# Layer 3's normalisation in eight VectorE steps, and a newly planned order, in an eight-part decoder kernel

## The chip, the cores and the metric

The kernel runs on one core of a Trainium2 chip. The metric is the time of one execution on the device in microseconds (us), as the median of several runs. Five engines work side by side, each through its own queue in order: TensorE (PE in the profile; PEld are its weight loads), VectorE (DVE), ScalarE (ACT), GpSimd (POOL) and SyncE (SP, which here only issues DMAs). The kernel before takes 1987.3 us (three runs, 1986.98 to 1990.2).

## The reference

x holds 128 batches of 64 tokens of 128 numbers, and a context of the same shape. Four layers follow one another; each adds an attention on the context and then a feed-forward part to x, and both read layer-normalised x:

```
x = x + L0_xattn(norm(x), ctx)   16 heads, softmax
x = x + L0_ffn(norm(x))          8 experts, gated by thresholded softmax
x = x + L1_xattn(ctx, norm(x))   16 heads, relative bias, softmax
x = x + L1_ffn(norm(x))          1 of 2 experts and a shared one, relu
x = x + L2_xattn(norm(x), ctx)   16 heads, masked products without softmax
x = x + L2_ffn(norm(x))          1 of 7 experts and a shared one, swiglu
x = x + L3_xattn(norm(x), ctx)   1 head; its result is normalised, scaled, shifted
x = x + L3_ffn(norm(x))          attention in which 2 of 4 experts give Wq, Wk, Wv
```

The changed code is the end of L3_xattn. With y the attention's result, mu and var its mean and variance over 128 numbers, gamma and beta two rows of weights:

```
x = x + (y - mu) * rsqrt(var + 1e-5) * gamma + beta
```

## The kernel before, in words

**Tiles.** The 8192 tokens are 16 groups of 512. The x of a group stays in SBUF as `xg[g]`, 128 partitions by 4 tiles (t) by 128 numbers. All arithmetic is in float32. The layers' parts are functions that append operations for one group: `attention` (layers 0 to 2), `l0f`, `l1f`, `route`, `shared`, `block`, `gather` (layer 2's feed-forward part, in two halves of 12 and 4 groups, with expert blocks gathered through DRAM), `l3x` (layer 3's attention, one call per group), `mix` and `l3f` (layer 3's feed-forward part, with weights chosen per batch; `load` on L1723 fetches those of a batch by DMA from SP).

**How the order comes about.** `op` appends an operation (a few instructions on one engine) to a `Plan`: the engine, a duration that the author gives in us, what it reads and writes, a priority. `alt` names another engine that may do it. `Plan.order` then works as a list scheduler: for each engine it looks at the ready operations, takes those that could start within `WINDOW` of the earliest, and of them the one of lowest priority; it compares the engines' choices by start (plus `ALT` times the duration where there is an alternative), books the engine and the buffer slot, and goes on. The priority is that of the group and stage plus a number from the table `PRI`, by the operation's name. `spec` gives how many buffers of a kind there are; an operation that needs one waits for a free slot. `port=True` says that a VectorE operation is to be planned only once POOL is free. The durations decide nothing but this order; each engine then runs its queue in it, and semaphores hold an instruction until its inputs are there.

**Around the change.** In `l3x` the values come out of two PSUM banks (`av`, L1538), are scaled into `y` (a buffer of kind "o", L1550), and `stats` (L536, L538) takes mean and variance of y on VectorE. `pow_rs` (L544, L545) makes rs = (var + eps)^-0.5 on POOL. Then, before the change, come: `norm`, four TENSOR_SCALARs on VectorE (L1562), y = (y - mu) * rs, one per tile; a product with gamma over the whole group on POOL (L1570); `add_row` (L610), x + beta, on POOL or VectorE; the sum x + y on POOL (L1574); and `stats` of the new x, for layer 3's feed-forward part. L1464 (in `gather`), L1399 (in `shared`) and L1078 (in `l0f`) are SCALAR_TENSOR_TENSORs on VectorE in the same shape, out = (in0 op scalar) op in1: L1464 takes both tensors from SBUF, L1399 and L1078 one from PSUM, and the four of an L1078 row add into the same tile of x one after another. L779 is the maximum over scores, L794 their subtraction on POOL, L785 the exponential, L809 the transposes of the scores, L821 the product with the values, L755 the scores, L1734 the projections with the chosen weights. L1199 to L1244 are the steps of routing (`r2` to `r5`), L1625 to L1637 the choice of experts in layer 3 (`choose`).

Of the kernel before, what the change touches and what calls it, by code (L numbers as in the profile page):

```python
# [16 lines left out]
ALU = mybir.AluOpType  # L17
# [3 lines left out]
P = 128  # L21
# [44 lines left out]
SKEW, SKEW3, ALT, WINDOW = 15.0, 12.0, 1.160527449, 0.268996472  # L66
# [5 lines left out]
    "block0 block <lambda> 4": -4, "block0 block tr 0": 37, "block0 dma fn 4": 30.5,  # L72
    "block0 swiglu <lambda> 0": 3.5, "block0 swiglu <lambda> 1": 35.5, "block0 swiglu <lambda> 2": -1,
    "block0 swiglu down 0": 20, "block1 block <lambda> 1": 13.5, "block1 block <lambda> 4": -12.5,
    "block1 block tr 0": -22.5, "block1 dma fn 4": 71, "block1 swiglu <lambda> 0": 4,
    "block1 swiglu <lambda> 1": 41, "block1 swiglu <lambda> 2": -32, "block1 swiglu down 0": 1,
    "gather0 gather <lambda> 3": 3.5, "gather0 gather fn 2": 6.5, "gather0 stats fn 2": -0.5,
    "gather1 gather <lambda> 3": 78, "gather1 gather fn 2": 29.5, "gather1 stats fn 2": -3.5,
    "l0f copy_out fn 1": 3, "l0f l0f <lambda> 0": 9, "l0f l0f <lambda> 1": 9.5, "l0f l0f <lambda> 2": -145,
    "l0f l0f acc 2": -123.5, "l0f l0f eb 0": 46.5, "l0f l0f g1 2": 43.5, "l0f l0f g2 2": 41.5,  # L80
    "l0f ln_xn fn 1": 17.5, "l0f logits fn 0": 18.5, "l0f pow_rs fn 3": -4, "l0f stats fn 2": -39,
    "l0f transpose4 fn 0": 59.5, "l1f add_row <lambda> 3": 12.5, "l1f copy_out fn 1": -43.5,
    "l1f l1f <lambda> 0": 196, "l1f l1f <lambda> 2": 55.5, "l1f l1f <lambda> 3": 48, "l1f l1f choose 2": 11.5,
    "l1f l1f down 0": 360, "l1f l1f relu 1": 32, "l1f ln_xn fn 1": -12, "l1f logits fn 0": 5, "l1f pow_rs fn 3": 7,
    "l1f stats fn 2": 0.5, "l1f transpose4 fn 0": 45.5, "l3f0 attend av 0": 41.5, "l3f0 attend tr 0": -4.5,
    "l3f0 copy_out fn 1": -52, "l3f0 dma fn 4": -9.5, "l3f0 exp_ <lambda> 1": 25, "l3f0 fill_kbd fn 4": 56,
    "l3f0 l3f <lambda> 1": 2, "l3f0 l3f <lambda> 2": 17, "l3f0 l3f <lambda> 3": 106, "l3f0 l3f b_v 3": 51.5,
    "l3f0 l3f evac 1": -131, "l3f0 l3f load 4": -2, "l3f0 l3f project 0": -36.5, "l3f0 l3f put 2": -15,
    "l3f0 maximum fn 2": 40, "l3f0 normalise fn 2": 4, "l3f0 out_proj <lambda> 2": 36, "l3f0 out_proj fn 0": 11,
    "l3f0 scores fn 0": -58, "l3f0 shift fn 3": -1, "l3f1 attend av 0": 1, "l3f1 attend tr 0": -22,  # L90
    "l3f1 copy_out fn 1": 8.5, "l3f1 dma fn 4": -3, "l3f1 exp_ <lambda> 1": 14, "l3f1 fill_kbd fn 4": -18,
    "l3f1 l3f <lambda> 1": -2, "l3f1 l3f <lambda> 2": -13.5, "l3f1 l3f <lambda> 3": 4, "l3f1 l3f b_v 3": 9.5,
    "l3f1 l3f evac 1": 12.5, "l3f1 l3f load 4": -13.5, "l3f1 l3f project 0": -58, "l3f1 l3f put 2": -8,
    "l3f1 maximum fn 2": 4, "l3f1 normalise fn 2": -2, "l3f1 out_proj <lambda> 2": 4, "l3f1 out_proj fn 0": -4.5,
    "l3f1 scores fn 0": -26, "l3f1 shift fn 3": -6.5, "l3x0 add_row <lambda> 3": 8, "l3x0 copy_out fn 1": -36,
    "l3x0 dma fn 4": 61.5, "l3x0 l3x <lambda> 1": 166, "l3x0 l3x <lambda> 2": -5.5, "l3x0 l3x <lambda> 3": -10.5,
    "l3x0 l3x av 0": 28.5, "l3x0 l3x norm 2": -21.5, "l3x0 l3x sc 0": 7, "l3x0 l3x sums 2": 33,
    "l3x0 l3x tr 0": -17.5, "l3x0 ln_xn fn 1": 14, "l3x0 pow_rs fn 3": 12, "l3x0 stats fn 2": 9,
    "l3x0 transpose4 fn 0": 15, "l3x1 add_row <lambda> 3": 3.5, "l3x1 copy_out fn 1": -38, "l3x1 dma fn 4": 97,
    "l3x1 l3x <lambda> 1": 36.5, "l3x1 l3x <lambda> 2": 8, "l3x1 l3x <lambda> 3": -2, "l3x1 l3x av 0": 13.5,  # L100
    "l3x1 l3x sc 0": 26, "l3x1 l3x sums 2": -28.5, "l3x1 l3x tr 0": 7.5, "l3x1 ln_xn fn 1": -1,
    "l3x1 pow_rs fn 3": -3, "l3x1 stats fn 2": -1, "l3x1 transpose4 fn 0": -1, "mix0 add_row <lambda> 3": 26.5,
    "mix0 copy_out fn 1": -64, "mix0 ln_xn fn 1": -3.5, "mix0 mix <lambda> 0": 54.5, "mix0 mix <lambda> 1": 18.5,
    "mix0 mix <lambda> 2": -29.5, "mix0 mix b3mm 0": 37.5, "mix0 mix choose 2": 81, "mix0 mix put 2": 27.5,
    "mix0 mix spread_ 0": 101, "mix0 mix weigh 2": -76, "mix0 pow_rs fn 3": -17.5, "mix0 transpose4 fn 0": 38,
    "mix1 add_row <lambda> 3": 42, "mix1 copy_out fn 1": -14.5, "mix1 ln_xn fn 1": 3.5, "mix1 mix <lambda> 0": 16,
    "mix1 mix <lambda> 1": 10.5, "mix1 mix <lambda> 2": -26.5, "mix1 mix b3mm 0": 1.5, "mix1 mix choose 2": 5.5,
    "mix1 mix put 2": 28, "mix1 mix spread_ 0": 15.5, "mix1 mix weigh 2": -25.5, "mix1 pow_rs fn 3": 2.5,
    "mix1 transpose4 fn 0": -0.5, "route copy_out fn 1": -98.5, "route dma fn 4": 0.5, "route ln_xn fn 1": 51.5,
    "route pow_rs fn 3": 13, "route route <lambda> 1": 2, "route route <lambda> 2": -25,  # L110
    "route route <lambda> 3": 48.5, "route route count 0": -3, "route route r2 2": -22, "route route r3 2": 8,
    "route route r4 2": 11.5, "route route r5 2": -1.5, "route route take 2": -4.5, "route stats fn 2": -19.5,
    "route transpose4 fn 0": 7, "shared0 copy_out fn 1": 10.5, "shared0 ln_xn fn 1": 10.5,
    "shared0 shared fn 2": 11.5, "shared0 swiglu <lambda> 0": 11, "shared0 swiglu <lambda> 1": 8.5,
    "shared0 swiglu <lambda> 2": 7, "shared0 swiglu down 0": 20.5, "shared0 transpose4 fn 0": 3.5,
    "shared1 copy_out fn 1": -16, "shared1 ln_xn fn 1": 24, "shared1 shared fn 2": -7,
    "shared1 swiglu <lambda> 0": 11, "shared1 swiglu <lambda> 1": -2.5, "shared1 swiglu <lambda> 2": 1,
    "shared1 swiglu down 0": 6.5, "shared1 transpose4 fn 0": 21.5, "table0 table <lambda> 0": 26,
    "table0 table b1 2": -3.5, "table0 table b2 2": 28, "table1 table <lambda> 0": 16, "table1 table b1 2": 2,
    "table1 table b2 2": 9.5, "x0 add_row <lambda> 3": 27, "x0 attend av 0": -6, "x0 attend tr 0": 9.5,  # L120
    "x0 attention <lambda> 2": -1.5, "x0 attention <lambda> 3": 26, "x0 copy_out fn 1": -102, "x0 dma fn 4": 504.5,
    "x0 exp_ <lambda> 1": -9, "x0 fill_kbd fn 4": -5, "x0 ln_xn fn 1": 19.5, "x0 maximum fn 2": 70,
    "x0 normalise fn 2": -88.5, "x0 out_proj <lambda> 2": -40.5, "x0 out_proj fn 0": -25.5, "x0 pow_rs fn 3": 4,
    "x0 proj <lambda> 0": 32.5, "x0 proj fn 1": -32, "x0 scores fn 0": 12, "x0 shift fn 3": -2,
    "x0 stats fn 2": -30, "x0 transpose4 fn 0": 10, "x0 vproj evac 1": -2, "x0 vproj fn 0": 73,
    "x1 attend av 0": 33, "x1 attend tr 0": 6.5, "x1 attention <lambda> 2": -35, "x1 attention <lambda> 3": 11,
    "x1 copy_out fn 1": -28.5, "x1 dma fn 4": 501.5, "x1 exp_ <lambda> 1": 10, "x1 fill_kbd fn 4": 5,
    "x1 ln_xn fn 1": 95.5, "x1 maximum fn 2": 10.5, "x1 normalise fn 2": -46.5, "x1 out_proj <lambda> 2": -103,
    "x1 out_proj fn 0": -1, "x1 pow_rs fn 3": 2, "x1 proj <lambda> 0": 24, "x1 proj fn 1": -1,
    "x1 scores fn 0": 83.5, "x1 shift fn 3": -14, "x1 stats fn 2": -15.5, "x1 transpose4 fn 0": 8,  # L130
    "x1 vproj evac 1": -1, "x1 vproj fn 0": 9.5, "x2 add_row <lambda> 3": 0.5, "x2 attention <lambda> 2": -46,
    "x2 attention <lambda> 3": 90.5, "x2 copy_out fn 1": -11.5, "x2 dma fn 4": 506, "x2 fill_kbd fn 4": 3.5,
    "x2 ln_xn fn 1": -3, "x2 out_proj <lambda> 2": -34, "x2 out_proj fn 0": -0.5, "x2 pow_rs fn 3": 8,
    "x2 product fn 0": -45, "x2 proj <lambda> 0": -13, "x2 proj fn 1": -9.5, "x2 scores fn 0": -13,
    "x2 stats fn 2": -15.5, "x2 transpose4 fn 0": 29, "x2 vproj_by_batch evac 2": -93.5,
    "x2 vproj_by_batch fn 0": -44, " b2_row b2_row 2": 2.5, " dma fn 4": 497, " lambda <lambda> 0": 32.5,
    " lambda <lambda> 2": -29.5, " lambda <lambda> 3": 14.5, " rel_mm rel_mm 0": -11.5,
# [162 lines left out]
def kernel(ctx: ExitStack, tc: tile.TileContext, a: dict, out: bass.AP):  # L300
# [93 lines left out]
    def g4(ap):  # L394
        return ap.rearrange("p (t d) -> p t d", t=TP)
# [1560 lines left out]
```

## Time and profile before

| what | us |
|---|---|
| median of three runs | 1987.3 |
| the profiled execution's own time | 1991.25 |
| its span, first to last instruction | 1989.5 |
| PE busy | 1811.3 |
| VectorE busy | 1546.2 |
| ScalarE busy | 1084.5 |
| POOL busy | 1022.3 |
| `norm`, L1562, 64 instructions, VectorE | 26.5 |
| product with gamma, L1570, 16 instructions, POOL | 20.5 |
| sum into x, L1574, 16 instructions, POOL | 20.3 |
| all bn_stats of x, L536, 512 instructions, VectorE | 110.5 |

Busy times of different engines overlap; one engine's busy time can't exceed the span. The page's second part gives busy tenths in 40 slices, each some 50 us: layers 0 to 2 fill roughly the first 1200 us, the expert blocks the next 300, layer 3 runs from about 1500 to the end. A row of the timeline names start, length, engine, line, operation, output<-inputs, shapes and how many instructions are merged, and in brackets for how long the engine had been idle and what ended that. Its length runs from the first start to the last end, so four instructions of 343 ns may take 1.13 us together: one starts before the one ahead has fully ended.

### The profile page before, as it was taken

How to read it: one execution, taken by the hardware profiler on the slowest of the kernel's cores; microseconds unless marked ns; L12 is line 12 of the kernel's file. 1: busy time of each engine (PE TensorE's matmuls, PEld its weight loads, DVE VectorE, ACT ScalarE, POOL GpSimd, SP SyncE). 2: the span in 40 equal slices, each digit the busy share in tenths (PEclk: the TensorE clock that was granted, in tenths of full speed). 3: DMA queues.
4: the chain of work that ended last, by engine and by line, in shares of the span. 5: the costliest groups of instructions: out<-in, count | busy, mean ns of one | idle time of the engine just before them, and what ended most of it. 6: DMA issues, size and time to landing. Idle time of an engine off the chain costs nothing.

```text
span 1989.5 us, 66420 instructions
## 1 busy us (share of the span) xinstructions
PE 1811.3 (91%) x27506; PEld 1306.3 (66%) x27506; DVE 1546.2 (78%) x4023; ACT 1084.5 (55%) x2032; POOL 1022.3 (51%) x1331
## 2 busy tenths in 40 slices
PE   6878999999999999999999999999999897888886
PEld 5544756665765666765666677878756676677665
DVE  5989897878798987798887865354577877988776
ACT  2544755555655564556564554344455666765664
POOL 4635745554555664457654471020388767755231
PEclk8989999999999999999999999999999999998898
DMA  6200001011011010001101012444424576545561
GB/s 187 79 13 27 27 26 30 13 30 41 19 34 46 24 35 29 27 26 50 29 25 33 22 37 84 124 136 122 119 74 124 153 237 198 173 148 167 174 196 55
DMA packets 139229, 158.73 MB, mean 80 GB/s; under 512 B 40836, under 2 KB 98096, under 8 KB 138928
## 3 DMA queue, kind: packets, MB, share of 16 engines
q1 hardware_dynamic: 134832, 146.09, 24.2%
q0 software_dynamic: 4096, 8.40, 1.4%
q8 instruction: 216, 3.54, 0.8%
q14 instruction: 85, 0.70, 0.1%
HBM read 121.66 MB, written 15.99 MB: 69 GB/s over the span
## 4 chain that ended last, share of the span: by engine, by line
PE 50%; DVE 25%; POOL 7%; issue 7%; ACT 5%; DMA 4%; SPq 2%; POOLq 0%; DVEq 0%; ACTq 0%
PE b L1353 8%; PE b L1144 6%; PE b L809 5%; DVE x L1078 4%; POOL s L794 4%; DVE mx L779 4%; PE S L755 4%; PE b L1125 4%; PE b L1382 4%; PE b L1068 3%; PE b L638 3%; PE b L1734 3%; PE b L821 2%; PE b L864 2%; DVE s L967 2%
## 5 line engine op out<-in xcount | busy, mean ns | idle before, releaser
L794 POOL TENSOR_TENSOR s<-s,mx 128x512 f32<-128x512 f32 x320 | 324.0, 1047 | 224.1 <-DVE mx L779 190.5
L593 ACT COPY p<-b 128x512 f32<-128x512 f32 x370 | 199.4, 591 | 143.2 <-PE b L809 128.2
L809 PE MATMUL b<-ident,s 128*128 128x128 f32 x1536 | 217.1, 291 | 45.9 <-ACT s L785 33.7
L785 ACT ACTIVATE s<-s 128x2048 f32<-128x2048 f32 x96 | 183.8, 1914 | 114.2 <-POOL s L794 84.2
L809 PEld LDWEIGHTS b<-ident,s 128*128 128x128 f32 x1536 | 180.2, 149 | 91.0 <-ACT s L785 55.2
L563 ACT ACTIVATE xn<-x,nmr,rstd 128x128 f32<-128x128 f32 x472 | 194.4, 487 | 26.8 <-POOL nmr L548 25.2
L1078 DVE SCALAR_TENSOR_TENSOR x<-b,gt,x 128x128 f32<-128x128 f32 x512 | 177.8, 347 | 30.5 <-PE b L1068 14.3
L544 POOL TENSOR_SCALAR ve<-mv 128x4 f32<-128x4 f32 x144 | 34.8, 242 | 319.4 <-DVE mv L538 304.8
L755 PE MATMUL S<-kbd,q 32*64 32x256 f32 x4096 | 152.8, 404 | 42.6 <-DMA kbd<-k 20.4
L1144 PEld LDWEIGHTS b<-fw,hbig 128*128 128x128 f32 x1536 | 180.6, 195 | 10.4 <-issue 9.4
L1144 PE MATMUL b<-fw,hbig 128*128 128x128 f32 x1536 | 186.3, 279 | 0.0
L779 DVE TENSOR_REDUCE mx<-s 128x32 f32<-128x2048 f32 x80 | 181.8, 2274 | 3.6 <-ACT s L1786 2.9
L1370 DVE TENSOR_TENSOR hbig<-fm,b 128x256 f32<-128x256 f32 (+2 forms) x180 | 85.4, 487 | 102.0 <-ACT fm L1365 75.1
L1134 ACT ACTIVATE hbig<-b,cols 128x512 f32<-128x512 f32 x164 | 111.3, 685 | 82.8 <-PE b L1125 81.8
L1068 PE MATMUL b<-mats,fx 128*128 128x512 f32 x256 | 140.5, 632 | 1.9 <-DVE x L1078 1.5
L545 POOL TENSOR_TENSOR rstd<-ve,mhalf 128x4 f32<-128x4 f32 x128 | 133.6, 1044 | 10.6
L755 PEld LDWEIGHTS S<-kbd,q 32*64 32x64 f32 x4096 | 82.1, 137 | 83.2 <-DMA kbd<-k 19.2
L1353 PE MATMUL b<-fx,hbig 128*128 128x256 f32 (+1 forms) x528 | 129.1, 393 | 4.7 <-ACT fx L1441 1.0
L1365 ACT ACTIVATE fm<-b 128x256 f32<-128x256 f32 (+2 forms) x180 | 76.7, 438 | 101.0 <-PE b L1353 91.9
L821 PEld LDWEIGHTS b<-p,vaug 128*32 128x32 f32 x6144 | 97.1, 111 | 50.6 <-issue 23.5
L821 PE MATMUL b<-p,vaug 128*32 128x64 f32 x6144 | 123.3, 225 | 6.5 <-issue 3.6
L1125 PE MATMUL b<-fm,fw 128*128 128x512 f32 x256 | 125.1, 606 | 0.6 <-DVE x L1078 0.3
(292 smaller groups left out, 3870.2 us busy)
## 6 DMA issues: line engine op xcount, KB each, us to landing
fw<-in_l_w SPq DMA_DIRECT2D x64, 384.0 KB
vaug<-in_l_w SPq DMA_DIRECT2D x64, 384.0 KB
hbig<-in_l_w SPq DMA_DIRECT2D x44, 544.0 KB
c<-in_ctxT SPq DMA_DIRECT2D x64, 256.0 KB
kbd<-k SPq DMA_DIRECT2D x256, 64.0 KB
q<-xs_d SPq DMA_DIRECT2D x44, 128.0 KB
ys_d<-o SPq DMA_DIRECT2D x44, 128.0 KB
x<-in_x SPq DMA_DIRECT2D x32, 128.0 KB
```

Of the source, the lines that this page charges most:

```text
L563: A.activation(y[:, t, :], xg[g][:, t, :], AF.Identity, bias=nmr[:, g, n], scale=rstd[:, g, n])
L593: A.copy(tl(dst), tl(b))
L755: T.matmul(ps[64 * i : 64 * i + 64, r, u * 256 : u * 256 + 256], lhsT=qT[row, 64 * b : 64 * b + 64], rhs=kbd[row, :, 64 * b : 64 * b + 64] ...
L779: V.tensor_reduce(tl(mxr), heads(y), AX.X, ALU.max)
L794: G.tensor_tensor(y, y, bc(tl(mxr)[:, h], 2, [P, n, S]), ALU.subtract)
L809: T.transpose(tl(b)[:, r * P : (r + 1) * P], tl(s)[:, c : c + P], ident)
L821: T.matmul(tl(po)[32 * r : 32 * r + 32, c : c + 64], lhsT=vaugs[kv.slot][:, w0 : w0 + 32], rhs=tl(ps[p])[:, r * P + 64 * i : r * P + 64 * ...
L1068: lambda t=t, u=u, pe=pe: T.matmul(tl(pe), lhsT=tl(xnT)[:, t * P : (t + 1) * P], rhs=mats[:, M_E0 + 4 * u : M_E0 + 4 * u + 4, :], start=Tr ...
L1078: V.scalar_tensor_tensor(xg[g][:, t, :], tl(pe)[:, e * D : (e + 1) * D], w[:, t, 4 * u + e : 4 * u + e + 1], xg[g][:, t, :], ALU.mult, ALU ...
L1125: lambda n=n, src=src, ph=ph: T.matmul(tl(ph), lhsT=fw[:, n * P : (n + 1) * P], rhs=tl(src), start=True, stop=True),
L1144: T.matmul(tl(py)[:, t * P : (t + 1) * P], lhsT=tl(hs[n])[:, t * P : (t + 1) * P], rhs=w2f[:, n, :], start=(n == 0), stop=(n == 11),)
L1353: T.matmul(tl(ps)[0:n, at : at + m], lhsT=w()[:, off + c * P : off + c * P + n], rhs=tl(xT)[:, 0:m], start=True, stop=True,)
```

## The change

First, the end of `l3x`. The product with gamma and the sum into x leave POOL. `norm` is now eight SCALAR_TENSOR_TENSORs on VectorE, two per tile: y = (y - mu) * gamma, then x = y * rs + x. The row beta is added to x ahead of it. The norm writes x and y, is planned at 1.75, and no longer waits for POOL in the plan.

```diff
+        add_row(g, R_BETA, pri)
+
         def norm():
             for t in range(TP):
-                V.tensor_scalar(
-                    g4(tl(y))[:, t, :], g4(tl(y))[:, t, :], mv3[:, g, t, 0:1], rs3[:, g, t : t + 1],
-                    ALU.subtract, ALU.mult,
+                y_, x_ = g4(tl(y))[:, t, :], xg[g][:, t, :]
+                V.scalar_tensor_tensor(
+                    y_, y_, mv3[:, g, t, 0:1], rows[:, R_GAMMA : R_GAMMA + D], ALU.subtract, ALU.mult
                 )
-
-        op(DVE, 1.3, norm, r=[R3, M3], w=[y], pri=pri, port=True)
-        op(
-            POOL, 1.27,
-            lambda: G.tensor_tensor(g4(tl(y)), g4(tl(y)), bc(rows[:, R_GAMMA : R_GAMMA + D], 1, [P, TP, D]), ALU.mult),
-            r=[W["rows"]], w=[y], pri=pri,
-        )
-        add_row(g, R_BETA, pri)
-        op(POOL, 1.27, lambda: G.tensor_tensor(xg[g], xg[g], g4(tl(y)), ALU.add), r=[y], w=[X[g]], pri=pri)
+                V.scalar_tensor_tensor(x_, y_, rs3[:, g, t : t + 1], x_, ALU.mult, ALU.add)
+
+        op(DVE, 1.75, norm, r=[R3, M3, W["rows"]], w=[y, X[g]], pri=pri)
         stats(g, pri)
```

Second, the durations that the plan is given (m is 4 for most calls of route):

```diff
-        op(DVE, 1.1 + 0.45 * m, r2, r=[C], w=[rt], pri=pri)
+        op(DVE, 1.1 + 0.65 * m, r2, r=[C], w=[rt], pri=pri)
-        op(DVE, 0.2 + 0.8 * m, r3, w=[rt, RUN[half]], pri=pri - 1)
+        op(DVE, 0.2 + 1.0 * m, r3, w=[rt, RUN[half]], pri=pri - 1)
-        op(DVE, 0.7 + 0.4 * m, r4, r=[rank, W["misc2"]], w=[rt], p=[POS[half]], pri=pri - 1)
+        op(DVE, 0.6 + 0.2 * m, r4, r=[rank, W["misc2"]], w=[rt], p=[POS[half]], pri=pri - 1)
-        op(DVE, 1.4 + 0.2 * m, r5, w=[rt, *WSH[g0 : g0 + m]], pri=pri)
+        op(DVE, 1.1 + 0.1 * m, r5, w=[rt, *WSH[g0 : g0 + m]], pri=pri)
-        op(PE, 1.0, av, r=[pT, cv], w=pos_, hold=[y], pri=pri, mode="v")
+        op(PE, 0.65, av, r=[pT, cv], w=pos_, hold=[y], pri=pri, mode="v")
-        op(DVE, 4.2, choose, r=[W["rows"], C], w=[sel, pg], pri=pri)
+        op(DVE, 2.7, choose, r=[W["rows"], C], w=[sel, pg], pri=pri)
-                op(SP, 0.95, load, r=[TAB3[g // GATE]], w=[wt], pri=pri - 1, lat=3.5, after=[*mark["l1f"], *mark["x2"]])
+                op(SP, 0.95, load, r=[TAB3[g // GATE]], w=[wt], pri=pri - 1, lat=4.3, after=[*mark["l1f"], *mark["x2"]])
-            op(ACT, 0.5, evac, r=[b, *VA], p=[va], hold=[kv], pri=pri, alt=[(DVE, 0.5)])
+            op(ACT, 0.6, evac, r=[b, *VA], p=[va], hold=[kv], pri=pri, alt=[(DVE, 0.5)])
```

Third, the numbers of buffers and of the planner. In `spec`, q goes from 2 to 4, k from 3 to 2, o from 3 to 2, fm from 4 to 3, p from 5 to 4, mb from 3 to 4, mx from 12 to 16, st from 4 to 18. Every entry of `PRI` is new (252 entries before, 244 after); two lines of some 100 show the kind:

```diff
-SKEW, SKEW3, ALT, WINDOW = 15.0, 12.0, 1.160527449, 0.268996472
+SKEW, SKEW3, ALT, WINDOW = 15.0, 12.0, 1.255146523, 0.172540063
...
-    "l3x0 l3x av 0": 28.5, "l3x0 l3x norm 2": -21.5, "l3x0 l3x sc 0": 7, "l3x0 l3x sums 2": 33,
+    "l3x0 l3x av 0": 13.5, "l3x0 l3x norm 2": 8, "l3x0 l3x sc 0": -35, "l3x0 l3x sums 2": 14.5,
```

The priorities of the DMAs of context, masks and x (`x0 dma`, `x1 dma`, `x2 dma` and `dma`) go from about 500 to about 735. With these numbers the order of the instructions on every engine and in every queue is made anew.

## The prediction

> **What bounds the kernel now.** I read the page's busy line and slices first, then busy time by stretches, then what TensorE waits for, and last single rows in order of time.
>
> ```profile
> span 1989.5 us, 66420 instructions
> PE 1811.3 (91%) x27506; PEld 1306.3 (66%) x27506; DVE 1546.2 (78%) x4023; ACT 1084.5 (55%) x2032; POOL 1022.3 (51%) x1331
> ...
> PE   6878999999999999999999999999999897888886
> ```
>
> TensorE (PE) is busy for 91% of the span: a full TensorE with gaps at both ends. As long as its work stays the same, at most 1989.5 - 1811.3 = 178 us can be won. The stretches say where the gaps lie (columns: stretch, length, busy PE, PEld, DVE, ACT, POOL, granted clock, DMA share, GB/s).
>
> ```profile
> 1200.00:1300.00 100.00, 98.83 (x893) 78.66 (x892) 45.98 (x127) 40.10 (x94) 8.60 (x14) 1.00 0.36 107
> ...
> 1500.00:1600.00 100.00, 87.36 (x682) 67.54 (x680) 79.35 (x328) 62.06 (x144) 79.89 (x114) 0.95 0.51 144
> 1600.00:1700.00 100.00, 84.94 (x1713) 69.00 (x1713) 78.41 (x211) 63.29 (x136) 68.41 (x82) 0.95 0.66 211
> 1700.00:1800.00 100.00, 84.25 (x2024) 69.70 (x2025) 91.46 (x242) 68.27 (x137) 66.34 (x84) 0.97 0.55 176
> 1800.00:1900.00 100.00, 82.12 (x1937) 69.18 (x1939) 76.13 (x164) 60.10 (x102) 45.39 (x49) 0.90 0.54 171
> ```
>
> TensorE idles 43.5 us before 200, 40.6 from 200 to 1200, 6.1 from 1200 to 1500, 61.3 from 1500 to 1900 and 27.2 in the last 90: layer 3, where the edited step runs (1498 to 1814), holds a third of all gaps, and the tail a seventh. What ended TensorE's waits from 1500 to 1830, the longest five (columns: waiting tile and line, releaser, total us, times, longest):
>
> ```profile
> PE S L755 <- DMA kbd<-k: 5.4, 3, 3.6
> PE S L755 <- DVE s L1778: 5.0, 5, 1.5
> PE b L1382 <- DVE hbig L1370: 3.1, 3, 2.1
> PE b L809 <- ACT p L593: 3.1, 6, 1.9
> PE b L1734 <- DVE tn L841: 2.4, 1, 2.4
> ```
>
> Over all rows of that answer VectorE (DVE) ends 24.5 of the 48.9 idle us there, half. GpSimd (POOL) ends 0.7. So time taken from POOL buys little directly, and time put on VectorE is paid at some 50%.
>
> **The step itself.** Its three old parts, undisturbed, and the three prices for the new one:
>
> ```profile
> 1552.66 1.11 DVE L1562 TENSOR_SCALAR o<-o,mv,rs 128x128 f32<-128x128 f32 x4
> ...
> 1553.85 1.27 POOL L1570 TENSOR_TENSOR o<-o,rows 128x512 f32<-128x512 f32 x1 [2.89 <-DVE o L1562]
> ...
> 1555.19 1.27 POOL L1574 TENSOR_TENSOR x<-x,o 128x512 f32<-128x512 f32 x1
> ```
>
> ```profile
> 500.63 1.51 DVE L1078 SCALAR_TENSOR_TENSOR x<-b,gt,x 128x128 f32<-128x128 f32 x4
> ...
> 1439.21 1.13 DVE L1464 SCALAR_TENSOR_TENSOR x<-k,tok,x 128x128 f32<-128x128 f32 x4
> ...
> 1690.35 3.94 DVE L1464 SCALAR_TENSOR_TENSOR x<-k,tok,x 128x128 f32<-128x128 f32 x4
> ...
> 1690.92 2.60 POOL L610 TENSOR_TENSOR x<-x,rows 128x512 f32<-128x512 f32 x2
> ```
>
> *Removed.* Per group 1.11 us of VectorE and two POOL products; from the first start (1552.66) to the last end (1556.46) 3.80 us. The 64 TENSOR_SCALARs hold 26.5 us of VectorE in all, 8.7 over 16 x 1.11, since some were stretched. POOL loses 20.5 + 20.3 = 40.8 us, and two hand-overs between engines, for which POOL waited 14.0 us and VectorE 3.3.
>
> *Added.* Eight SCALAR_TENSOR_TENSORs per group. Independent ones (L1464) take 1.13 us for four: pitch (1.13 - 0.343)/3 = 0.262. Where each reads what the one before wrote (L1078), four take 1.51: pitch (1.51 - 0.347)/3 = 0.388. The new loop alternates: the second of a pair reads the y that the first wrote, the next pair is independent. So 4 x 0.388 + 3 x 0.262 + 0.343 = 2.68 us, at least 7 x 0.262 + 0.343 = 2.18 if nothing is held. I take 2.68, since L1078 is the nearest row with such a dependence. VectorE then holds 16 x 2.68 = 42.9 us, 16.4 more than now; with stalls like the present 8.7, 25.1 more. From 1500 to 1830 it would be busy some 293 to 302 us of 330 instead of 276.8.
>
> *On the path.* The chain of work that ended last, cut to 1490 to 1835, holds 7.9 us of L1562 (2.3% of 345) and 5.1 of the two POOL products: 13.0. The new step, on that chain in the same share, holds 7.9 x 42.9/26.5 = 12.8. I cost the fused step at 0: what the two POOL products give back, VectorE takes. Ends: -13 if it leaves the chain, +25 if every added VectorE us shows. The 3.3 us in which stats waited for L1574 go; late next are the stats themselves, in order behind the longer norm on VectorE.
>
> *The wait it adds.* The norm now writes x, so it waits for the beta row (L610, 1.27 us, on POOL for 62 of 80). Behind it on VectorE stand stats, maxima and evacuations. The row needs only the old x and is now ahead of the norm; POOL's power for rs (L545, 1.05 us), which the norm needs in any case, covers most of it. Price 0, or 16 x 1.27 = 20 if beta comes last each time; that lies within the +25.
>
> *The shared port.* The four-instruction row at 1690 took 3.94 us instead of 1.13 while two POOL sums ran; 1.60 and 2.31 stand in two other groups. The L1399 form, whose one tensor is in PSUM, never passed 353 ns. The Trainium skill (SBUF — State Buffer, Who interferes with whom) gives the reason, and it speaks against this edit: a VectorE instruction with two tensors in SBUF contends with a GpSimd instruction that reads SBUF, and the later one stands still till the other is done. By that rule the eight new instructions all are exposed, and one POOL sum met per group would add an estimated 16 x 1.27 = 20 us; by the rows of L1464 (4.5 us of stalls on 18.1 of work) the new step would gather 11, with 40.8 us less of POOL to meet. The sum above uses 8.7, the present step's.
>
> **The new order.** Every instruction after the start may move, on SP's and POOL's queues too; no row prices that, so I bound it. Ends: all gaps after 1500 closed (-88), or layer 3's VectorE-ended waits doubled (+24). For a gain speak the planner's new costs, checked against rows: choose ran from 1582.72 to 1585.29, 2.57 (old cost 4.2, new 2.7); the running sums of routing 596.35 to 600.47, 4.1 (3.4, now 4.2); r4 604.87 to 605.94, 1.1 (2.3, now 1.4); r2 592.65 to 596.4, 3.7 (2.9, now 3.7); sixteen av matmuls 0.60 to 0.84 (1.0, now 0.65); weight loads on the chain 4.7 to 5.7 (3.5, now 4.3). All move toward the trace, and the chain's longest pieces in layer 3 are such loads. Against it stands one: the norm is planned at 1.75 less 0.09 = 1.66, and I expect 2.68. So VectorE runs 1.0 late per group, 16 in all; at 50% this costs 8 us. I take a quarter of the 88.5 idle us after 1500 as regained, 22: between nothing and all, nearer nothing since the old order came of the same planner and waits are many and small (none above passes 5.4 us in sum). The changed buffers (q, mb, mx, st more; k, o, fm, p fewer) I cost at 0: no wait above is for a free buffer by name; each costs at most one such wait (2 us) per group in a stage if the cover goes.
>
> **Sum.** 0 - 22 + 8 = -14 us. The profiled execution took 1991.25 (span 1989.5 and 1.75 around it), so 1977.3; the median of the runs, 1987.3, is 4.0 below that execution, and the same step gives 1973.
>
> **Rivals.** *A, the forecast (0.50):* layer 3's gaps shrink, 1973; its own range 1952 to 1983. *B, the whole order improves (0.08):* a third of the 84 idle us before 1200 goes as well, 1973 - 28 = 1945. For it: SP, priorities and buffers change everywhere; against it, 200 to 1200 is 96% busy. *C, the step doesn't shorten (0.08):* a POOL op met each time makes 2.68 + 1.27 = 3.95 against 3.80, and the order regains only that: 1987. *D, VectorE becomes the bound in layer 3 (0.34):* for it speak 91.46 us of 100 at 1700 to 1800 already, and a norm planned a third too short, so that queues behind it shift. Its price is the whole 25 us on VectorE, less the 3.3 of stats' waits that go, with nothing regained by the order: +22, 2009. It decides where the order regains less than what reaches TensorE of those 25: 12 us at the share of 50%, 25 at full share. Against it: VectorE still idles 28 us of the 330 in the sum above.
>
> **How the numbers follow.** About 0.2% (4 us, 1983.3 to 1991.3) is what a measurement here can tell from no change. Faster by more: A and B, 0.58; within: C, 0.08; slower: D, 0.34. The range 1948 to 2012 takes in A, C and the upper end of +25, and leaves out most of B and the worst of D, in which the order loses as well: some 0.2 together.
>
> **What would show it.** Right: eight instructions of some 2.7 us per norm, POOL near 981 us busy, VectorE near 1563 to 1571, TensorE's idle after 1500 down by 10 to 20 us. Wrong: a norm of 2.2 or of 4 us; VectorE over 95% busy between 1700 and 1800 with TensorE's waits on it grown; gaps that moved to the front. One thing would break the sum altogether: an order that changes the 200 to 1500 stretch by more than its 47 idle us suggest.

## The result and the profile after

The changed kernel takes 2000.9 us (median of seven runs, 1997.1 to 2008.2) where the kernel before takes 1987.3 on the same chip: ratio 1.0070, 95% interval 1.0051 to 1.0090, so 14 us slower where 14 us faster was forecast. The case that came nearest is rival D: VectorE's work in layer 3 is paid for. The profiled execution took 1997.25 us, 6.0 more than the profiled one of before, so the two profiles together show less than half of the 14 us. The page of after, busy times and TensorE's slices:

```profile
span 1995.5 us, 66520 instructions
...
PE 1810.9 (91%) x27506; PEld 1312.2 (66%) x27506; DVE 1582.0 (79%) x4090; ACT 1086.4 (54%) x2062; POOL 975.0 (49%) x1294
...
PE   7778999999999999999999999999988888787786
```

TensorE's work is what it was (1810.9 against 1811.3 us). POOL has lost 47.3 us, and VectorE has gained 35.8. The gaps stand where they stood, at both ends, but those at the back are deeper. The stretches, in the same columns as for the kernel before:

```profile
1400.00:1500.00 100.00, 90.48 (x545) 63.10 (x545) 73.31 (x266) 47.27 (x106) 61.83 (x85) 0.97 0.37 106
1500.00:1600.00 100.00, 82.33 (x799) 62.26 (x797) 87.30 (x332) 49.37 (x118) 64.48 (x100) 0.85 0.49 147
1600.00:1700.00 100.00, 86.57 (x1629) 72.06 (x1629) 82.17 (x204) 66.56 (x132) 36.56 (x46) 0.98 0.55 171
1700.00:1800.00 100.00, 77.08 (x1813) 64.39 (x1811) 90.34 (x221) 64.69 (x131) 60.36 (x76) 0.93 0.60 183
1800.00:1900.00 100.00, 80.12 (x1942) 68.54 (x1939) 88.71 (x206) 62.28 (x134) 45.10 (x56) 0.93 0.54 167
```

Add up TensorE's busy time to see where these 6 us went. At 1400 us the new kernel has done 1326.0 us of it and the old one 1314.6: it is 11.4 us ahead. At 1860 it has done 1708.7 against 1715.3: it is 6.5 behind. So 18 us were lost in these 460, most of them layer 3's, where VectorE was busy 388.0 us instead of 366.6. From 1400 to the end, the waits of TensorE that VectorE ended grew from 34.3 to 56.1 us, those that ScalarE ended from 24.6 to 33.9, and those that DMAs ended shrank from 23.5 to 10.7. The longest five from 1500 to 1830:

```profile
PE S L753 <- DVE s L1772: 6.3, 7, 1.5
PE b L1728 <- DVE x L891: 4.2, 1, 4.2
PE b L1380 <- DVE hbig L1368: 4.1, 2, 3.9
PE S L753 <- DMA kbd<-k: 3.4, 3, 1.4
PE b L819 <- DVE hbig L1368: 3.3, 1, 3.3
```

Four of the five name VectorE now (three did before), and three of these come down to a single wait of 3.3 to 4.2 us each: one operation of VectorE came late, once. The longest single wait in the five shown of before was 3.6, for a DMA. The two lines of the new step (busy us, mean ns of one):

```profile
L1566 DVE SCALAR_TENSOR_TENSOR x<-o,rs,x 128x128 f32<-128x128 f32 x64 | 31.2, 488 | 5.2 <-POOL rs L543 2.2
...
L1563 DVE SCALAR_TENSOR_TENSOR o<-o,mv,rows 128x128 f32<-128x128 f32 x64 | 26.4, 412 | 0.1
```

The rows add up to 57.6 us. Neighbours overlap and are counted twice there, as each starts before the one ahead has ended; with the overlaps counted once the step holds VectorE for some 53.7 us. Forecast were 42.9 bare and 51.6 with stalls. Undisturbed a norm takes 2.75 us from first start to last end (1558.21 to 1560.96), close to the 2.68 worked out. At the median lengths (346 and 352 ns) the two rows would add up to 64 x 0.346 + 64 x 0.352 = 44.7 us, so 12.9 us are stalls. One of the stretched norms, and who waits for it:

```profile
1581.41 1.27 POOL L608 TENSOR_TENSOR x<-x,rows 128x512 f32<-128x512 f32 x1
1581.51 1.32 DVE L1566 SCALAR_TENSOR_TENSOR x<-o,rs,x 128x128 f32<-128x128 f32 x1
...
1582.64 2.13 POOL L1698 TENSOR_TENSOR mats<-hbig,mats 128x512 f32<-128x512 f32 x2
1582.75 1.12 DVE L1563 SCALAR_TENSOR_TENSOR o<-o,mv,rows 128x128 f32<-128x128 f32 x1
...
1583.91 1.01 DVE L1566 SCALAR_TENSOR_TENSOR x<-o,rs,x 128x128 f32<-128x128 f32 x1
...
1585.00 1.31 POOL L608 TENSOR_TENSOR x<-x,rows 128x512 f32<-128x512 f32 x1
1585.22 1.23 DVE L1566 SCALAR_TENSOR_TENSOR x<-o,rs,x 128x128 f32<-128x128 f32 x1
...
1587.14 0.42 DVE L1368 TENSOR_TENSOR hbig<-fm,b 96x256 f32<-96x256 f32 x1
...
1587.61 0.38 PE L1380 MATMUL b<-hbig 128*128 128x128 f32 x1 [3.85 <-DVE hbig L1368]
```

Read it downwards. Each instruction takes 0.35 us alone. Four of the eight take 1.01 to 1.32, and each of them starts some 0.1 to 0.2 us after a POOL operation has begun (L1698's row holds two) and ends some 0.15 us after it: VectorE stands until POOL has done. Over all 64 of each line the longest take 1126 and 1391 ns, while the medians stay at 0.35 us: a minority of the instructions makes the stalls. The norm lasts from 1581.04 to 1587.11, 6.07 us. Directly behind it on VectorE stands L1368, and TensorE's matmul of L1380 waits 3.85 us for that. One stretched norm is a wait on TensorE in the very next operation.

### The profile page after: what moved, and what is told of

It is laid out like the page before. It is cut to its first block, busy times and chain, and to the rows that moved or that the text cites. A ratio compares the mean times of both kernels' runs of the same rounds, so it can differ in the third digit from the quotient of the medians.

```text
span 1995.5 us, 66520 instructions
## 1 busy us (share of the span) xinstructions
PE 1810.9 (91%) x27506; PEld 1312.2 (66%) x27506; DVE 1582.0 (79%) x4090; ACT 1086.4 (54%) x2062; POOL 975.0 (49%) x1294
## 3 DMA queue, kind: packets, MB, share of 16 engines
q1 hardware_dynamic: 134832, 146.09, 24.2%
## 4 chain that ended last, share of the span: by engine, by line
PE 48%; DVE 31%; POOL 6%; issue 6%; ACT 4%; DMA 3%; SPq 1%; POOLq 0%; DVEq 0%; ACTq 0%
PE b L1351 8%; PE b L1142 6%; PE b L807 5%; DVE x L1076 4%; PE b L1123 4%; PE b L1380 4%; DVE mx L777 4%; PE S L753 3%; POOL s L792 3%; DVE s L965 2%; PE b L819 2%; PE b L1066 2%; PE b L1728 2%; PE b L636 2%; PE b L581 2%
## 5 line engine op out<-in xcount | busy, mean ns | idle before, releaser
L783 ACT ACTIVATE s<-s 128x2048 f32<-128x2048 f32 x96 | 183.5, 1912 | 121.9 <-POOL s L792 95.4
L753 PE MATMUL S<-kbd,q 32*64 32x256 f32 x4096 | 147.8, 398 | 31.3 <-DVE s L1772 13.1
L1368 DVE TENSOR_TENSOR hbig<-fm,b 128x256 f32<-128x256 f32 (+2 forms) x180 | 85.8, 488 | 104.3 <-ACT fm L1363 77.1
L543 POOL TENSOR_TENSOR rstd<-ve,mhalf 128x4 f32<-128x4 f32 x128 | 133.5, 1043 | 10.7
L1247 POOL DMA_INDIRECT xs_d<-p,rt x64 | 63.3, 990 | 126.4 <-ACT p L561 102.4
```

What stands on the lines that cost most here:

```text
L753: T.matmul(ps[64 * i : 64 * i + 64, r, u * 256 : u * 256 + 256], lhsT=qT[row, 64 * b : 64 * b + 64], rhs=kbd[row, :, 64 * b : 64 * b + 64] ...
L783: op(ACT, 1.92, lambda: A.activation(tl(s), tl(s), AF.Exp), w=[s], pri=pri, mode="exp")
```

## The experiments

Two theories: **S**, the step costs the time, since VectorE's work in layer 3 grows; **O**, the step is nearly free, and the newly made order is worse on the chip. Ratios are to the kernel before on the same chip, with 95% intervals; busy times are those of one profiled execution each; 1 point, a hundredth of the ratio, is some 20 us.

**e1, the step alone.** Before's order, instruction for instruction; the eight instructions stand where the four stood, and the two POOL products are left out of POOL's queue, their sums being in the eight.

```diff
-                V.tensor_scalar(
-                    g4(tl(y))[:, t, :], g4(tl(y))[:, t, :], mv3[:, g, t, 0:1], rs3[:, g, t : t + 1],
-                    ALU.subtract, ALU.mult,
+                y_, x_ = g4(tl(y))[:, t, :], xg[g][:, t, :]
+                V.scalar_tensor_tensor(
+                    y_, y_, mv3[:, g, t, 0:1], rows[:, R_GAMMA : R_GAMMA + D], ALU.subtract, ALU.mult
+                )
+                V.scalar_tensor_tensor(x_, y_, rs3[:, g, t : t + 1], x_, ALU.mult, ALU.add)
...
+            lambda: None,
```

> The order of before, instruction for instruction, with the eight SCALAR_TENSOR_TENSORs in the place of the four TENSOR_SCALARs and without the two POOL products. Theory S (the step: VectorE pays): 16 norms grow from 1.11 us to 2.75 and more, some 26 us of added VectorE time with stalls, of which most reaches the end: 2003 to 2012. Theory O (the order: the step is free, the new plan is worse on the chip): within 0.3% of before, 1981 to 1993.

Measured: 1.0061 (1.0047 to 1.0075), +12 us, between the ranges of S and O. VectorE went up by 19.2 us to 1565.4, POOL down by 41.1. The step by itself brings nearly the whole loss, without any new order. Its rows:

```profile
L1566 DVE SCALAR_TENSOR_TENSOR x<-o,rs,x 128x128 f32<-128x128 f32 x64 | 26.5, 413 | 4.2 <-POOL rs L545 1.3
L1563 DVE SCALAR_TENSOR_TENSOR o<-o,mv,rows 128x128 f32<-128x128 f32 x64 | 25.3, 395 | 0.0
```

They add up to 51.8 us, 7.1 of them stalls. So in this order both the length of the step and VectorE's total came as forecast (51.6, and 1563 to 1571); what they cost did not.

**e2, half of the step in after's order** (first of the two instructions out).

```diff
-                V.scalar_tensor_tensor(
-                    y_, y_, mv3[:, g, t, 0:1], rows[:, R_GAMMA : R_GAMMA + D], ALU.subtract, ALU.mult
-                )
```

> The order of after, with only the second instruction of each pair: x = y * rs + x. The subtraction of the mean and the product with gamma are left out, so the norm is four instructions, about 1.1 us where the plan has 1.66. Theory S: some 35 us of VectorE time go (57.6 busy to about 22), and 70 to 90% of it shows: 1970 to 1980, below before. Theory O: at most half shows, and the new order stays at or above before: 1986 to 1999.

Measured: 0.9933 (0.9915 to 0.9951). Its norm holds 26.2 us in all, 1.64 a group: about what the order was planned for. VectorE is busy 1557.8 us, 24.2 less than in the changed kernel, and the time is 1.37 points, 27 us, less: theory S's range.

**e3, two loops:** four first steps, then four second ones, so that no instruction reads what the one just ahead of it wrote.

```diff
+            for t in range(TP):
+                y_, x_ = g4(tl(y))[:, t, :], xg[g][:, t, :]
                 V.scalar_tensor_tensor(x_, y_, rs3[:, g, t : t + 1], x_, ALU.mult, ALU.add)
```

> The order of after; the norm does its four first steps and then its four second ones, so that no instruction reads what the one ahead of it wrote: 7 x 0.262 + 0.343 = 2.18 us undisturbed instead of 2.75, 9 us less in all. Theory S: 1992 to 1994. Theory O: 1996 to 2001.

Measured: 1.0036 (1.0018 to 1.0054), between the ranges of S and O. The norm's rows shrink from 57.6 to 48.7 us, but part of that is overlap that is no longer counted twice: VectorE as a whole goes from 1582.0 to 1578.2. A third of a point comes back; still slower than before.

**e4, a third instruction per tile**, whose result nobody reads.

```diff
                 V.scalar_tensor_tensor(x_, y_, rs3[:, g, t : t + 1], x_, ALU.mult, ALU.add)
+                V.scalar_tensor_tensor(
+                    y_, y_, mv3[:, g, t, 0:1], rows[:, R_GAMMA : R_GAMMA + D], ALU.subtract, ALU.mult
+                )
```

> The order of after with a third instruction per tile, which writes the dead y again: twelve instead of eight, some 1.2 us more per norm undisturbed, 19 to 25 us in all with stalls. Theory S (share of 70 to 90%): 2015 to 2024. Theory O (share of half or less): 2003 to 2012.

Measured: 1.0233 (1.0211 to 1.0255), above what either theory gave. VectorE went up by 28.6 us and the time by 1.63 points, 32 us. With e2 this is a line: from four instructions per norm to twelve, in this order, VectorE grows by 52.8 us and the time by 3.0 points, 60 us (54 to 65). A microsecond put on VectorE by the norm costs 1.1 us here (1.0 to 1.2).

**e5, half of the step in before's order** (e1 without the first of each pair).

> The order of before, and in the norm's place only x = y * rs + x: four SCALAR_TENSOR_TENSORs, about 1.1 us as the TENSOR_SCALARs that they replace, and no POOL products. The subtraction of the mean and the product with gamma are left out. Together with the same norm in the order of after (0.9933 of before) it shows what the new order is worth when the norm is short. If the new order is worth what it is ahead by at 1400 us (11 us of TensorE work): 0.999 to 1.001 of before, 1989 to 1993. If the new order is worth nothing: 0.992 to 0.995, 1975 to 1981, all of the gain coming from the two POOL products that go.

Measured: 0.9951 (0.9929 to 0.9974), on another chip on which all times are some 50 us longer, so only the ratio counts. Together with e1 this splits the step: two POOL products and two hand-overs gone at nearly the same VectorE time (1547.5 against 1546.2) are worth 0.49 points, 10 us (5 to 14); the 17.9 us by which e1's VectorE stands above that cost 1.10 points, 22 us (17 to 27). It prices the order as well. With half of the step the new order differs from the old by -0.18 points (0.9933 against 0.9951), with the whole step by +0.09 (1.0070 against 1.0061); the intervals, some 0.3 wide each way, hold zero both times. Theory O falls: the order neither gained nor lost what can be measured. The half step in the new order takes about what the plan gives it (1.64 against 1.66), and even so the order is not clearly ahead.

**e6, the four old normalising instructions on ScalarE**, in before's order; two small POOL operations per group make the bias.

```diff
-                V.tensor_scalar(
-                    g4(tl(y))[:, t, :], g4(tl(y))[:, t, :], mv3[:, g, t, 0:1], rs3[:, g, t : t + 1],
-                    ALU.subtract, ALU.mult,
-                )
+                y_, n = g4(tl(y))[:, t, :], slice(t, t + 1)
+                A.activation(y_, y_, AF.Identity, bias=nmr[:, g, n], scale=rs3[:, g, n])
```

> The order of before and its three parts, but the four normalising instructions are ScalarE's (scale rs, bias -mean*rs) in the place of VectorE's, and two small POOL operations per group make the bias. If VectorE's time in layer 3 is what is paid for (theory S): 26.5 us of VectorE go and 16 x 1.7 = 27 us of ScalarE come, which is busy 60 to 68% there: 0.988 to 0.997 of before. If any engine's added time in this chain costs the same (theory O's reading: the order was packed around the old lengths): 1.000 to 1.008.

Measured: 1.0057 (1.0035 to 1.0080). VectorE fell by 23.1 us to 1523.1, ScalarE rose by 23.2 to 1107.6, and the kernel became 11 us slower. So S in its simple form, that VectorE's load sets the time, doesn't hold: unloading it gained nothing, although ScalarE is idle 45% of the span. One reading, argued and not shown: ScalarE's queue had no place kept for the 26.4 us, and what costs is whatever makes a queue late against an order packed around other lengths. A rival stands beside it: the two added POOL operations lie between rs and the norm, so that each norm starts later as well, and no run takes them away.

**e7 and e8, a quiet POOL in after's order.** In layer 3 POOL's row sums, its products with the experts' weights and its subtractions of the maximum become memsets of about the same length, which write SBUF and read nothing. In e7 all of each is replaced; in e8 each keeps a few columns of its work, so that its waits stay. Both leave the rest of these sums out of the result.

```diff
+    def quiet(*widths):
+        for w_ in widths:
+            G.memset(kinds["rt"][0][:, 0:w_], 0.0)
...
-            lambda e: (G if e == POOL else V).tensor_tensor(
+            lambda e: (quiet(400, 400, 200), G.tensor_tensor(
+                xg[g][:, :, 0:4], xg[g][:, :, 0:4], bc(rows[:, off : off + 4], 1, [P, TP, 4]), ALU.add
+            )) if e == POOL and off in (R_BETA, R_BO3) else
+            (G if e == POOL else V).tensor_tensor(
```

> The order of after, but in layer 3 POOL's sums with the rows beta and the last bias, its products with the experts' weights and its subtraction of the scores' maxima are memsets of about the same length, which write SBUF and read nothing. These sums, products and subtractions are left out of the result. If the stalls of the norm come from POOL reading SBUF while VectorE reads two tensors: the norm's busy time falls from 57.6 us to 44 to 49, and the whole to 0.993 to 1.001 of before. If POOL's being busy is enough: the norm stays at 54 to 60 us and the whole at 1.004 to 1.010.

> As e7, but every quietened POOL operation keeps a small part of its old work (4 of 128 columns of the row sums, one of 64 columns of the subtraction and of the products), so that who waits for whom stays as in after; the memsets fill up the old length. The rest of those sums, subtractions and products is left out of the result. If the gain of e7 came from POOL reading less: norm 45 to 48 us busy, time 0.990 to 0.996 of before. If it came from waits that e7 had loosened: norm 45 to 48 us all the same, time 1.001 to 1.008.

Measured: e7 0.9904 (0.9885 to 0.9923), faster than either range, and e8 0.9929 (0.9908 to 0.9949), as expected if reading is what stalls. In e7 some waits went too (TensorE's on ScalarE for L783's exponential shrank from 20.0 to 6.8 us after 1400; in e8 they are 14.7), so e8 counts. The groups of e8's norm:

```profile
L1577 DVE SCALAR_TENSOR_TENSOR x<-o,rs,x 128x128 f32<-128x128 f32 x64 | 23.1, 360 | 5.2 <-POOL rs L543 2.2
L1574 DVE SCALAR_TENSOR_TENSOR o<-o,mv,rows 128x128 f32<-128x128 f32 x64 | 22.1, 345 | 0.1
```

45.2 us instead of 57.6, with POOL as busy as in the changed kernel (971.3 against 975.0 us). The norm shown above, the eighth of its queue, with the same queue around it:

```profile
1579.25 1.24 POOL L607 MEMSET rt<- 128x400 f32 x3
1579.37 0.35 DVE L1577 SCALAR_TENSOR_TENSOR x<-o,rs,x 128x128 f32<-128x128 f32 x1
1579.64 0.35 DVE L1574 SCALAR_TENSOR_TENSOR o<-o,mv,rows 128x128 f32<-128x128 f32 x1
1580.02 0.35 DVE L1577 SCALAR_TENSOR_TENSOR x<-o,rs,x 128x128 f32<-128x128 f32 x1
...
1581.72 0.42 DVE L1379 TENSOR_TENSOR hbig<-fm,b 96x256 f32<-96x256 f32 x1
...
1582.19 1.60 PE L1391 MATMUL b<-hbig 128*128 128x128 f32 x12 [0.57 <-DVE hbig L1379]
```

Beside three memsets (1.24 us) every instruction keeps its 0.35. The norm takes 2.78 us (1578.91 to 1581.69), and TensorE waits 0.57 us where it waited 3.85. TensorE's waits that VectorE ended after 1400 are 40.5 us instead of 56.1.

**e9, the same quiet POOL in before**, as the measure of what quiet is worth without the change.

> The same quietening in before, with its order and its three-part step (whose two POOL products stay as they are). If the lock costs layer 3 something in any case and the change only shares in it: as much gain as e8 has against after. If the change is what brought VectorE under the lock: 0.995 to 1.000 of before, a third or less of e8's gain.

Measured: 0.9963 (0.9949 to 0.9977). The norm goes from 26.5 to 22.6 us. Quiet gains 0.37 points here and 1.41 in the changed kernel; the difference, 1.04 points with some 0.3 either way, is 21 us. The stalls outside the norm grew as well: when POOL is quiet the norm sheds 12.4 us in the changed kernel and 3.9 in before, the rest of VectorE 10.2 and 3.9. So the 21 us belong to the step and the new order together; the step alone (e1) with a quiet POOL was not run. With POOL quiet in both, the change would have been 0.34 points faster instead of 0.70 slower. One more reservation: zeros are multiplied further on in both, and TensorE's busy time falls in both, by 9 us in e8 and 12 in e9; about equal, so it should drop out of the difference, but that was not tried by itself.

**e10 to e12, orders searched anew.** All three have after's other durations and buffers, and a priority table of their own, found by a search over the planner. e10 has the old step of three parts, with its old durations. e11 has e3's step, planned at 2.75 instead of 1.66. e12 has e3's step as well, planned at 2.26 and only at moments at which POOL is planned idle.

e11's duration (the planner takes 0.09 off each):

```diff
-        op(DVE, 1.75, norm, r=[R3, M3, W["rows"]], w=[y, X[g]], pri=pri)
+        op(DVE, 2.84, norm, r=[R3, M3, W["rows"]], w=[y, X[g]], pri=pri)
```

> The three-part step of before, with the other new durations and buffers of after and a table of priorities searched for this step. If the fused step is what after loses by, an order of this kind without it is clearly ahead: 0.985 to 0.997 of before. If new orders as such bring nothing on the chip: 0.998 to 1.008.

> The fused step in its two loops (as in e3), planned at its measured 2.75, and a table of priorities searched for that. If the wrong duration in the plan was the fault: 0.985 to 0.996 of before. If the fault is the shared port, of which this plan knows nothing: 0.997 to 1.005, since e3 took 1.0036 in the old order.

> As e11, but the norm is planned at 2.26 and only for moments when POOL is free (port=True, as the four instructions of before were). If the port is the fault and a start beside an idle POOL is enough: 0.3% or more below e11, 0.984 to 0.995 of before. If POOL's later starts lock it all the same: level with e11.

Measured on one chip, on which before takes 2037.9 us: e10 0.9904 (0.9883 to 0.9926), e11 0.9888 (0.9864 to 0.9912), e12 0.9996 (0.9976 to 1.0016). e11 beats both kernels: 1.1 points under before, and 1.5 under e3, which has the same instructions in after's order. Its norm takes as long as e3's (49.1 us against 48.7); what differs is the order, in the length that it was planned for and in every priority. e12's expectation missed: planning the start for an idle POOL shortened the norm only from 49.1 to 46.2 us, and 46.2 is still 0.6 a group more than the 2.26 that this order knows of. e10 and e11 can't be told apart: with an order searched for each, the fused step is worth about as much as the old one. What these three can't show is how much of a point is the luck of one search, as each is a single order. e10 gained a point on before with the step and the norm's duration unchanged, so e11's lead over e3 can't be laid to the norm's planned length alone.

## Why the prediction was wrong, step by step

Forecast and result lie 28 us apart, and two terms of the sum make this up: the step, 0 in the sum and +12 us by e1, and the new order, -22 + 8 = -14 in the sum and +2 us (1.0070 against 1.0061, some 5 either way).

- **"I cost the fused step at 0: what the two POOL products give back, VectorE takes."** This step failed, by its price and not by its size. The products give back 10 us (e5 against before), near the 13.0 that was read from the chain. VectorE's time came as forecast in e1 (1565.4 us). But it takes 22 us (e1 against e5) where 12.8 was forecast, and 27 in the new order (changed kernel against e2). The 12.8 rests on the words "on that chain in the same share": 7.9 of the old norm's 26.5 us lay on the chain of work that ended last, 30%. In the same cut, 1490 to 1835, the two new lines make up 8.5% of that chain in e1, 29 us or more than half of their 51.8, and 9.3%, 32 us, in the changed kernel. Added work did not keep the share of the old.
- **"Time put on VectorE is paid at some 50%."** The share of TensorE's waits that VectorE ends is no price. (The rows of that answer add up to 23.5 us, not 24.5; of the 48.9 that is still half.) Measured, added VectorE time costs 122% (e1 against e5: 22 us for 17.9), 113% (changed kernel against e2: 27 for 24.2) and 113% (e4: 32 for 28.6). Each alone is good to some 20 to 30 points, so all three are far above 50% and none is clearly above 100%. TensorE's waits on ScalarE grew too, from 24.6 to 33.9 us after 1400, as if lateness in one queue were passed on to others; no run tests that path.
- **"I take a quarter of the 88.5 idle us after 1500 as regained, 22."** This step failed as well. Nothing was regained: new and old order agree within some 0.3 points with the half step and with the whole one, and TensorE's idle time after 1500 rose from 88.5 to 101.1 us instead of falling by 10 to 20. With the half step, whose norm fits the plan, the ratios leave the new order 4 us ahead, some 6 either way, so the norm's wrong duration does not explain the missing 22. One premise was weak: of the weight loads on the chain those into vaug take 4.7 to 5.7 us, but those into fw in layer 3 take 2.6 to 4.2, around the old cost. That such a gain can be had is what e10 shows: an order searched with the new durations and buffers for the old step is 20 us under before. Why this order has none of it stays open. It did gain 11.4 us before 1400, 3.6 of them before 200, and gave them back in layer 3 in the profiled execution.
- **The norm planned a third too short, "at 50% this costs 8 us".** The fault was seen, its size not: with its stalls a norm holds VectorE for some 3.5 us instead of the planned 1.66, so that VectorE comes some 30 us late in all, not 16. What this alone costs no run separates. The same instructions in an order planned for their length run 1.5 points faster (e11 against e3), but that order is also another draw of the search.
- **Stalls "like the present 8.7".** The undisturbed 2.68 was right (2.75), and so was the 8.7 in before's order (7.1 in e1). In the new order the stalls were 12.9 us, nearer the 11 that the prediction worked out from the rows of L1464 and set aside; and by e8 the rest of VectorE sheds another 10.2 when POOL is quiet (22.6 in all, less 12.4), which no term of the sum held.
- The Trainium skill (SBUF — State Buffer, Who interferes with whom) says that a VectorE instruction with two inputs in SBUF contends with GpSimd instructions that read SBUF, and not with those that only write it. Both halves hold here: beside POOL operations that read, the instructions take 1.01 to 1.32 us, beside memsets 0.35. The estimate of 20 us that the prediction made by that rule, one sum met per norm, is above the 12.9 found in the norm; the 21 us of e8 and e9 are another quantity, time of the whole kernel.
- **Rival D** had the sign and named the cause, VectorE's added time, at a chance of 0.34. It priced +22 and 14 was measured: the removal gave 10 back, of which the rival counted 3.3. Its condition, "the order regains less than what reaches TensorE", was met. But of the signs, VectorE over 95% busy between 1700 and 1800 did not come (90.34), and e6 speaks against its name: with 23.1 us taken off VectorE the kernel got no faster.
- Right: POOL near 981 (981.2 in e1, 975.0 in the changed kernel), eight instructions of some 2.7 us undisturbed, and the beta row, for which the norm shows no wait by name (the only one is 2.2 us, for rs). VectorE's 1563 to 1571 was right for the step and too low for the changed kernel (1582.0): there four more row sums went to VectorE (22 instead of 18, 4.3 us), which no step had counted, and the stalls were longer.

## What to carry to other kernels

The share of a wait or of a chain that an engine holds now is no price for work added to it. A kernel with one instruction added and one with an instruction taken out, in the same order, measure that price in two runs: here it was about the whole of the added time, and not half. In an order that is planned by hand-given durations, price an added operation with the stalls that the rows nearest to it show, and give the plan that length: the same eight instructions were 0.4 points slower than before in an order planned for 1.66 us and 1.1 points faster in one planned for 2.75. This is a hint and no proof, since each order is one draw of a search, and a search for the old step gained as much. Before moving a sum from GpSimd to VectorE, look at which GpSimd operations read SBUF at that time: in the norm shown, an instruction with two inputs in SBUF that started beside one of them ended only some 0.15 us after it, up to 1 us late each time.

## What the runs showed of the hardware

- Chains of short VectorE instructions are hit again and again: 0.35 us of work took 1.01 to 1.32 us in four of the eight instructions of the norm shown. The two POOL sums beside it kept their lengths (1.27 and 1.31 us; the mean of all 58 is 1.28), so that VectorE paid.
- SCALAR_TENSOR_TENSOR of 128x128: a second one that reads what the first wrote starts 0.39 us behind it (1558.92 to 1559.31), an independent one 0.27 (1559.31 to 1559.58).
- The granted clock from 1500 to 1600 differs between kernels with the same work for TensorE: 0.81 at 78.2 us of TensorE busy (e4), 0.85 at 82.3 (changed kernel), 0.95 at 87.4 (before), 0.97 at 86.4 (e2). It does not simply follow the busy time: 0.91 at 79.0 (e10) and 0.88 at 86.1 (e7) stand across. What sets it was not tried.
